# GpSimd's gathers in an edge-message kernel: issued when their buffers are free, no longer when TensorE passes given points

## The chip, the cores and the metric

The kernel runs on one core of one Trainium2 chip. The metric is device time in microseconds (us), the median of several runs. A core has five engines that work side by side, each through its own instructions in a fixed order: TensorE (PE: matrix products; PEld is its weight load), VectorE (DVE), ScalarE (ACT), GpSimd (POOL) and SyncE (SP, which only starts transfers). They wait for each other through semaphores. Transfers (DMA) run on 16 DMA engines and are started by SP, ACT or POOL.

## The reference

It is one layer of a graph network over 12,500 nodes of 32 features and 400,000 edges, which are sorted by their target node:

```python
h = jnp.maximum(_layernorm(x, axis=-1), 0.0)            # 12500 x 32
e_feat = jnp.concatenate([h[src], h[dst], edge_attr])   # per edge: 3 x 32 = 96
v = relu(e_feat @ W1 + b1) @ W2 + b2                    # 96 -> 64 -> 32
x_cand = jax.ops.segment_max(v, dst, num_segments=num_nodes)
out = x + jnp.maximum(x_cand, h)
```

## The kernel before, in words

**Tiling.** The edges are cut into four stripes of 100,000, and the four stripes lie on the 128 partitions, 32 features each. A chunk is 512 edges of every stripe, so 2048 edges; there are 196 chunks (`NCH`). A chunk has 16 columns (`K`) of 128 edges. Before the main loop the kernel normalises the nodes and writes `h` to memory as `h_d`, together with `q_d`, its product with the target part of `W1`.

**Two ways to fetch the source rows `h[src]`.** Of a chunk's 16 columns, 12 are fetched by POOL: one indirect DMA per column (`DMA_INDIRECT gh<-h_d,src_i`, line 179), which reads 128 rows of 128 bytes. The other 4 columns (`MM`) are looked up by TensorE instead: `tile(c, m)` multiplies a one-hot matrix `hot` with the node table `hs` in 14 matmuls of 448 columns (line 344), then DVE multiplies the result with a mask (`one<-pv,mask`, line 351) and takes a maximum (`gm<-one`, line 352). In 34 of the chunks (`MMX`) TensorE looks up a fifth column, `tile(c, MM)`, and POOL fetches 11.

**Buffers of the gathers.** POOL's columns land in tiles `gh` of three columns each, four tiles per chunk. The pool `gathered` has 14 such tiles. DVE turns each with one `STREAM_TRANSPOSE ht<-gh` (`to_features`, line 368), and after that the tile may be filled again: a gather's first column waits for the transposition of the tile 14 places earlier. Each gather also waits for the landing of the gather eight places earlier, since eight semaphores (`DMASW0` to `DMASW7`) take turns.

**The main loop.** It goes over pairs of chunks, 97 rounds. With c the pair that is finished, a = c+2 and b = c+3 are the chunks whose columns are fetched by TensorE in that round. On TensorE a round is, in this order: `ph<-ea` (the products with `edge_attr`, line 773), `ph<-of,qf` (with the target's part), `ph<-ht` (with the transposed source rows, `rows_into`), the transpositions `pv<-ident,sb` of the pair before (line 669), the tiles a1, a2, a3, the second layer `pv<-hid` (line 807), the product `pv<-so,last` that picks the last edge of each node (line 686), the tiles b0 to b3 (and the fifth tile, if there is one), and tile a0 of the next round. DVE transposes the gathered columns tile by tile between its work on TensorE's tiles. In one round it transposes eight `gh` tiles (a1 to a3, b0 to b3 and the next round's a0), and the next round's `rows_into` multiplies what it has transposed.

**What sets the order.** The kernel runs under a schedule written by hand: each engine carries out its instructions in the order of the program text. POOL's queue has nothing but gathers in the main loop. The gathers of chunks a+2 and a+3 stand at the end of a round's text, but POOL runs ahead of that as far as its waits allow. Those waits are the buffers, the eight semaphores, and, before the change, points of TensorE's order: `passes(round, name, ins)` remembers the instruction after which TensorE has passed a point, and `hold(c, i, ins)` makes gather i of chunk c wait for one. The table `HELD` names the points: of the 24 gathers of a pair every second one has a point. The first four points (`b1`, `b2`, `b3`, `n0`: the tiles b1, b2, b3 and the next a0) are of three pairs back, the other eight (`ea`, `ht`, `tr`: the three blocks of that name and the transpositions; `a1`, `a2`, `a3`; `lv`, which is the product of line 686; `b0`) of two pairs back. A second, short table `SOON` names points for the first gathers of chunks 3, 4 and 5; those points lie in the prologue.

Of the kernel before, what the change touches and what calls it, by code (L numbers as in the profile page):

```python
# [37 lines left out]
K = C // D  # L38
# [10 lines left out]
MM = 4  # L49
# [14 lines left out]
LATE = NCH - 8  # L64
PIECE = 2 * A0
GP = 3
HELD = {0: (3, 'b1'), 2: (3, 'b2'), 4: (3, 'b3'), 6: (3, 'n0'), 8: (2, 'ea'), 10: (2, 'ht'), 12: (2, 'tr'), 14: (2, 'a1'), 16: (2, 'a2'), 18: (2, 'a3'), 20: (2, 'lv'), 22: (2, 'b0')}
BANKS = 7
SOON = {(3, 0): 'a0', (3, 6): 'a2', (4, 0): 'a3', (4, 6): 'b0', (5, 0): 'b1', (5, 6): 'b2'}
ROUND = 12582912.0  # L70
# [13 lines left out]
def gnn_kernel(ctx, tc, x, src, src_mm, src_x, src_t, dst, dst_ext, lo, lo_c, ends_b, edge_attr, weights, w1, w2, b2, out):  # L84
# [88 lines left out]
    def gather(c):  # L173
        n = min(K - MM * (c in MMC), (SE - c * C) // D) - (c in MMX)
        parts = []
        for k in range(0, n, SOME):
            parts.append(gathered.tile([P, SOME, D], F32, name="gh"))
            for i in range(min(SOME, n - k)):
                ins = nc.gpsimd.indirect_dma_start(  # L179
                    out=parts[-1][:, i, :], out_offset=None, in_=h_d[:, :],  # L180
                    in_offset=bass.IndirectOffsetOnAxis(ap=src_i[:, c, k + i:k + i + 1], axis=0))
                hold(c, k + i, ins)
        return parts
# [33 lines left out]

    def hold(c, i, ins):

        at = HELD.get(i + c % 2 * (K - MM))  # L220
        if at and c // 2 - at[0] >= 0:
            waiting.append((ins, (c // 2 - at[0], at[1])))
        if (c, i) in SOON:
            waiting.append((ins, (0, SOON[c, i])))

    waiting = []
# [336 lines left out]
    with tc.tile_pool(name="edges", bufs=3) as pool, tc.tile_pool(name="edges_ps", bufs=1, space=PSUM) as ps:  # L563
# [290 lines left out]
        for c in range(0, NCH - 4, 2):  # L854
# [14 lines left out]
            if c == LATE + 2:  # L869
                ea = pool.tile([P, LOAD * C], F32, name="ea", bufs=2)  # L870
# [123 lines left out]
        c = NCH - 4  # L994
# [192 lines left out]
```

## Time and profile before

| | |
|---|---|
| median of three runs | 3579.48 us (3571.26 to 3581.6) |
| time of the profiled execution | 3575.96 us |
| its span, first to last instruction | 3574.1 us |
| mean granted TensorE clock | 0.944 |
| busy: PE, DVE, POOL, ACT | 3241.7, 2223.2, 2207.4, 1578.5 us |

The views quoted further on are these. The page of the profile gives each engine's busy time, the chain of work that ended last, and groups of instructions: engine, operation, output and inputs, count, then busy time, mean duration in ns, and the idle time of the engine just before them with what ended it. A row of the timeline has start, duration, engine, line and operation, and in brackets the idle time before it. A view by line has count and durations (min/median/max in ns). A view by stretches has, for each window, the length, the busy time of PE, PEld, DVE, ACT and POOL with counts, the granted TensorE clock, the share of the DMA engines and GB/s.

### The profile page before, as it was taken

What the parts mean: (1) busy time and instruction counts of PE and PEld (TensorE: products, weight loads), DVE (VectorE), ACT (ScalarE), POOL (GpSimd) and SP (SyncE); (2) the same over time, 40 slices, a digit from 0 to 9 for tenths busy, and PEclk for the clock granted to TensorE, in tenths of its full rate; (3) what the DMA queues carried; (4) which work ended last, traced back from release to release, by engine and by line L of the source; (5) the groups of instructions that cost most, each with busy time, mean ns of one, the idle gap of its engine ahead of it and who ended that gap; (6) DMA issues with size and microseconds to landing.
All of it is one profiled execution on the core that took longest, in us unless ns stands there. A gap on an engine that the chain in (4) does not pass through costs nothing.

```text
span 3574.1 us, 55458 instructions
## 1 busy us (share of the span) xinstructions
PE 3241.7 (91%) x19141; PEld 2547.7 (71%) x19141; DVE 2223.2 (62%) x4215; ACT 1578.5 (44%) x2470; POOL 2207.4 (62%) x2337
## 2 busy tenths in 40 slices
PE   5899999989999998999999999989999999999987
PEld 3577777777777776777777767777777777777765
DVE  5456666666666666666666666656665666666655
ACT  3344444443534444444443434444444444444443
POOL 6666666665666666666666666666666666666662
PEclk8899999999999999999999999999999999999997
DMA  5322222222222222222222222222222222222222
GB/s 175 99 60 62 53 64 62 62 50 62 64 62 53 61 63 65 50 66 60 62 50 70 57 56 58 59 59 61 60 62 59 60 61 61 63 65 49 59 58 65
DMA packets 178819, 227.49 MB, mean 64 GB/s; under 512 B 109621, under 2 KB 150373, under 8 KB 165734
## 3 DMA queue, kind: packets, MB, share of 16 engines
q10 hardware_dynamic: 29828, 108.01, 9.6%
q0 software_dynamic: 74336, 38.21, 8.5%
q1 hardware_dynamic: 74370, 77.70, 7.0%
q8 instruction: 151, 2.47, 0.3%
q14 instruction: 134, 1.10, 0.1%
HBM read 212.23 MB, written 11.46 MB: 63 GB/s over the span
## 4 chain that ended last, share of the span: by engine, by line
PE 81%; issue 10%; DVE 6%; another core or an unknown queue 2%; SPq 1%; DMA 1%; ACT 1%; DVEq 0%; ACTq 0%
PE pv L344 60%; PE ph L773 10%; PE pv L686 4%; PE pv L669 3%; PE pv L807 3%; DVE hot L304 1%; DVE one L351 1%; DVE last L650 1%; DVE sm L815 1%; DMA top_d<-wo 0%; DVE ht L368 0%; SPq L616 0%; SPq L707 0%; SPq L625 0%
## 5 line engine op out<-in xcount | busy, mean ns | idle before, releaser
L179 POOL DMA_INDIRECT gh<-h_d,src_i x2291 | 2169.8, 947 | 1296.3 <-issue 560.0
L344 PE MATMUL pv<-hs,hot 128*128 128x448 f32 x10752 | 2373.0, 378 | 97.5 <-issue 83.9
L344 PEld LDWEIGHTS pv<-hs,hot 128*128 128x128 f32 x10752 | 2089.1, 196 | 345.7 <-issue 159.7
L351 DVE TENSOR_TENSOR one<-pv,mask 128x448 f32<-128x448 f32 x768 | 472.3, 615 | 1219.7 <-remote 464.7
L798 ACT ACTIVATE hid<-ph,wt 128x512 f32<-128x512 f32 x392 | 250.0, 688 | 1124.6 <-remote 498.2
L352 DVE TENSOR_REDUCE gm<-one 128x32 f32<-128x448 f32 x768 | 476.2, 620 | 26.5
L304 DVE TENSOR_TENSOR hot<-kb,consts 128x1024 fp32r<-128x1024 f16 (+1 forms) x379 | 447.5, 1199 | 0.0
L318 ACT ACTIVATE hot<-away,ones 128x512 fp32r<-128x512 f32 x582 | 421.6, 724 | 45.0 <-remote 26.1
L317 ACT ACTIVATE away<-kb,key_n 128x512 f32<-128x512 f16 x582 | 416.0, 715 | 0.0
L692 ACT ACTIVATE wo<-pv 128x256 f32<-128x256 f32 x95 | 36.6, 385 | 631.2 <-remote 439.2
L815 DVE TENSOR_TENSOR_SCAN sm<-pb,sm,pv 128x512 f32<-128x512 bf16 x195 | 243.6, 1249 | 16.5 <-remote 9.0
L686 PEld LDWEIGHTS pv<-so,last 128*128 128x128 f32 x768 | 107.5, 191 | 159.5 <-issue 148.5
L773 PE MATMUL ph<-ht,wt 32*64 32x512 f32 x1568 | 197.3, 618 | 21.0 <-issue 13.0
L686 PE MATMUL pv<-so,last 128*128 128x256 f32 x768 | 148.6, 304 | 74.3 <-issue 67.7
L368 DVE STREAM_TRANSPOSE ht<-gh 128x96 f32<-128x96 f32 x774 | 207.4, 269 | 1.2
L661 ACT ACTIVATE sb<-sm,wt 128x512 f32<-128x512 f32 x196 | 138.1, 715 | 138.7 <-issue 87.6
L669 PEld LDWEIGHTS pv<-ident,sb 128*128 128x128 f32 x782 | 91.8, 150 | 120.3 <-issue 95.1
L773 PE MATMUL ph<-of,qf 32*64 32x512 f32 x1552 | 147.6, 600 | 19.6 <-issue 17.5
L669 PE MATMUL pv<-ident,sb 128*128 128x128 f32 x782 | 126.4, 298 | 30.4 <-issue 24.4
L773 PEld LDWEIGHTS ph<-ht,wt 32*64 32x64 f32 x1568 | 62.7, 135 | 114.1 <-issue 98.5
L642 ACT ACTIVATE of<-of,ones 128x512 f32<-128x512 f32 x194 | 140.6, 725 | 6.3
L641 ACT ACTIVATE of<-db,below 128x512 f32<-128x512 int32 x194 | 137.4, 708 | 0.0
(115 smaller groups left out, 1328.2 us busy)
## 6 DMA issues: line engine op xcount, KB each, us to landing
ea<-in_edge_attr SPq DMA_DIRECT2D x49, 1024.0 KB
db<-in_dst_ext ACTq DMA_DIRECT2D x48, 1024.0 KB
gh<-h_d,src_i POOLq DMA_INDIRECT x2291
pb<-pen_d ACTq DMA_DIRECT2D x48, 512.0 KB
kb<-key_d ACTq DMA_DIRECT2D x47, 512.0 KB
top_d<-wo SPq DMA_DIRECT2D x752, 3.0 KB
qf<-q_d SPq DMA_DIRECT2D x392, 16.0 KB
q_d<-qs SPq DMA_DIRECT2D x6, 512.0 KB
```

The costliest lines, as they stand in the source:

```text
L179: ins = nc.gpsimd.indirect_dma_start(out=parts[-1][:, i, :], out_offset=None, in_=h_d[:, :], in_offset=bass.IndirectOffsetOnAxis(ap=src_i[ ...
L304: nc.vector.tensor_tensor(hot_of(c)[:, start:stop], keys[c][:, None, :].to_broadcast([P, n, MM * P]), key_ps[:, start:stop, None].to_broad ...
L317: nc.scalar.activation(away, keys[c], AF.Square, bias=key_n[:, k:k + 1])
L318: nc.scalar.activation(hot_of(c)[:, k], away, AF.Relu, bias=ones, scale=-1.0)
L344: ins = nc.tensor.matmul(po, hot[k], hs[:, part, k].rearrange("p f a -> p (f a)"), start=(k == 0 and part == 0), stop=(k == A1 - 1 and par ...
L351: nc.vector.tensor_tensor(one, of_group, mask[:, None, :].to_broadcast([P, D, A0]), op=ALU.mult)
L352: nc.vector.tensor_reduce(row, one, axis=AX.X, op=ALU.max)
L669: passes(c // 2 + 1, "tr", nc.tensor.transpose(px[:, j, :], sb[:, j * P:(j + 1) * P], ident))
L686: ins = nc.tensor.matmul(pw[:, x % n], last[x][:, j].rearrange("p s w -> p (s w)"), sos[x][0][:, j], start=(j == 0 and x < n), stop=(j == ...
L773: ins = nc.tensor.matmul(ph[s][x * HID:(x + 1) * HID], w[g], e[g], start=start, stop=stop)
L798: nc.scalar.activation(hid[k], of, AF.Relu, bias=b1c)
L815: nc.vector.tensor_tensor_scan(found[:, :n], loaded.pop(c)[2][:, :n], pv[:, :n], -LOW if before is None else before[:, C - 1:C], op0=ALU.a ...
```

## The change

The table `HELD` and the three lines of `hold` that use it are taken out. What is left of `hold` serves `SOON` alone.

```diff
-HELD = {0: (3, 'b1'), 2: (3, 'b2'), 4: (3, 'b3'), 6: (3, 'n0'), 8: (2, 'ea'), 10: (2, 'ht'), 12: (2, 'tr'), 14: (2, 'a1'), 16: (2, 'a2'), 18: (2, 'a3'), 20: (2, 'lv'), 22: (2, 'b0')}
...
     def hold(c, i, ins):
 
-        at = HELD.get(i + c % 2 * (K - MM))
-        if at and c // 2 - at[0] >= 0:
-            waiting.append((ins, (c // 2 - at[0], at[1])))
         if (c, i) in SOON:
             waiting.append((ins, (0, SOON[c, i])))
```

No instruction of any engine changes its place. What changes is what POOL waits for. In the middle of the program, the twelve gathers of one chunk stood so on POOL before (`DMASW` is the landing of the gather eight places back, `DVE` the buffer, `PE` the point of TensorE's order):

```order
L179 DMA gh_16348<-h_d_63,src_i_70 128x32 [waits DMASW0_49,DVE_49,PE_49]
L179 DMA gh_16348<-h_d_63,src_i_70 128x32 [waits DMASW1_49]
L179 DMA gh_16348<-h_d_63,src_i_70 128x32 [waits DMASW2_49,PE_49]
L179 DMA gh_16352<-h_d_63,src_i_70 128x32 [waits DMASW3_49,DVE_49]
L179 DMA gh_16352<-h_d_63,src_i_70 128x32 [waits DMASW4_49,PE_49]
L179 DMA gh_16352<-h_d_63,src_i_70 128x32 [waits DMASW5_49]
L179 DMA gh_16356<-h_d_63,src_i_70 128x32 [waits DMASW6_49,DVE_49,PE_49]
```

And the same gathers on POOL now:

```order
L178 DMA gh_16348<-h_d_63,src_i_70 128x32 [waits DMASW0_49,DVE_49]
L178 DMA gh_16348<-h_d_63,src_i_70 128x32 [waits DMASW1_49]
L178 DMA gh_16348<-h_d_63,src_i_70 128x32 [waits DMASW2_49]
L178 DMA gh_16352<-h_d_63,src_i_70 128x32 [waits DMASW3_49,DVE_49]
L178 DMA gh_16352<-h_d_63,src_i_70 128x32 [waits DMASW4_49]
L178 DMA gh_16352<-h_d_63,src_i_70 128x32 [waits DMASW5_49]
L178 DMA gh_16356<-h_d_63,src_i_70 128x32 [waits DMASW6_49,DVE_49]
```

Every second gather has lost its wait for PE; the first of every tile still waits for its buffer. Over the whole program POOL's waits for PE go from 1146 to 11. At the start, in chunks 4 and 5, POOL's order before was:

```order
L179 DMA gh_801<-h_d_63,src_i_70 128x32 [waits DMASW0_49,PE_49]
L179 DMA gh_805<-h_d_63,src_i_70 128x32 [waits DMASW1_49]
L179 DMA gh_805<-h_d_63,src_i_70 128x32 [waits DMASW2_49,PE_49]
L179 DMA gh_805<-h_d_63,src_i_70 128x32 [waits DMASW3_49]
L179 DMA gh_809<-h_d_63,src_i_70 128x32 [waits DMASW4_49]
```

And now it is:

```order
L178 DMA gh_801<-h_d_63,src_i_70 128x32 [waits DMASW0_49]
L178 DMA gh_805<-h_d_63,src_i_70 128x32 [waits DMASW1_49]
L178 DMA gh_805<-h_d_63,src_i_70 128x32 [waits DMASW2_49]
L178 DMA gh_805<-h_d_63,src_i_70 128x32 [waits DMASW3_49]
L178 DMA gh_809<-h_d_63,src_i_70 128x32 [waits DMASW4_49,PE_49]
```

Before, chunk 4's last tiles waited for `ea` and `ht` of the first round, and the points of `SOON`, which lie earlier, came for nothing behind them; now the first gather of chunk 5 waits for its point of `SOON`. The instructions of PE, DVE, ACT and SP, and what they wait for, are the same in both programs; 48 of PE's signals, which only POOL read, are gone.

## The prediction

> **What bounds the kernel now.** I read the page first: the busy times, the chain that ended last, then the groups that the change touches.
>
> ```profile
> span 3574.1 us, 55458 instructions
> ...
> PE 3241.7 (91%) x19141; PEld 2547.7 (71%) x19141; DVE 2223.2 (62%) x4215; ACT 1578.5 (44%) x2470; POOL 2207.4 (62%) x2337
> ...
> PE 81%; issue 10%; DVE 6%; another core or an unknown queue 2%; SPq 1%; DMA 1%; ACT 1%; DVEq 0%; ACTq 0%
> ...
> L179 POOL DMA_INDIRECT gh<-h_d,src_i x2291 | 2169.8, 947 | 1296.3 <-issue 560.0
> ...
> L368 DVE STREAM_TRANSPOSE ht<-gh 128x96 f32<-128x96 f32 x774 | 207.4, 269 | 1.2
> ```
>
> TensorE is busy for 91% and makes 81% of the chain; POOL is on the chain with nothing. POOL's output is read by one thing alone, the 774 transpositions, and the last row's last number is DVE's idle time in front of all of them together: 1.2 us. So no transposition waits for a gather in a way that counts, and a gather that comes earlier can save 1.2 us at the most.
>
> Next, what POOL waits for, longest first, and how far it is ahead. The second fence is the view by line of the first 1800 us: gathers issued, transpositions done, fifth columns done.
>
> ```profile
> POOL gh L179 <- issue: 560.0, 1760, 3.4
> POOL gh L179 <- remote: 289.8, 181, 3.5
> POOL gh L179 <- PE pv L344: 238.8, 147, 4.7
> POOL gh L179 <- PE pv L686: 64.4, 34, 2.1
> POOL gh L179 <- PE ph L773: 58.6, 33, 6.1
> ```
>
> ```profile
> L179 POOL DMA_INDIRECT gh<-h_d,src_i x1156: 939/947/1463, 53.2 to 1799.0; - x193
> ...
> L368 DVE STREAM_TRANSPOSE ht<-gh x380: 233/268/280, 92.4 to 1795.0; 128x96 f32<-128x96 f32 x190
> ...
> L352 DVE TENSOR_REDUCE gh<-one x17: 619/620/621, 382.1 to 1774.8; 128x32 f32<-128x448 f32 x17
> ```
>
> By 1800 us 380 tiles had been turned, with 380 x 3 - 17 = 1123 gathered columns in them, and 1156 had been issued: POOL was 33 columns or 11 tiles ahead, of 14 that exist. The points of TensorE's order do hold it: three tiles stand empty. Without them POOL fills all 14.
>
> **The change, part by part.** One pair from the middle, from the timeline (POOL and DVE):
>
> ```profile
> 1812.50 0.27 DVE L368 STREAM_TRANSPOSE ht<-gh 128x96 f32<-128x96 f32 x1
> 1812.79 0.95 POOL L179 DMA_INDIRECT gh<-h_d,src_i  x1 [0.30 <-issue]
> 1815.46 0.94 POOL L179 DMA_INDIRECT gh<-h_d,src_i  x1 [1.72 <-remote]
> ...
> 1824.04 0.62 DVE L351 TENSOR_TENSOR one<-pv,mask 128x448 f32<-128x448 f32 x1 [8.91 <-remote]
> 1824.28 0.94 POOL L179 DMA_INDIRECT gh<-h_d,src_i  x1 [1.62 <-remote]
> ...
> 1825.23 0.27 DVE L368 STREAM_TRANSPOSE ht<-gh 128x96 f32<-128x96 f32 x1
> ...
> 1833.22 0.95 POOL L179 DMA_INDIRECT gh<-h_d,src_i  x1 [1.75 <-PE pv L344]
> ```
>
> ```profile
> 1807.94:1819.66 11.72, 10.61 (x60) 4.59 (x60) 6.99 (x16) 2.53 (x4) 7.87 (x9) 0.72 0.37 72
> 1819.66:1831.00 11.34, 11.34 (x70) 9.41 (x69) 6.67 (x13) 5.09 (x8) 7.59 (x9) 0.99 0.31 88
> 1831.00:1844.30 13.30, 13.30 (x68) 12.46 (x67) 11.28 (x23) 8.30 (x13) 7.99 (x9) 1.00 0.23 57
> sum 36.36, PE 35.25 PEld 26.47 DVE 24.93 ACT 15.93 POOL 23.44; mean PE 11.75 PEld 8.82 DVE 8.31 ACT 5.31 POOL 7.81
> ```
>
> *When the gathers go.* A gather takes 0.947 us, and 0.30 us passes to the next even without a wait, so 1.25 us. The 24 of a pair need 30.0 of its 36.4 us, and 6.4 us are left as waits. Now they come as pauses of 1.6 to 1.75 us in many places. Afterwards only an empty tile lets POOL go on: eight transpositions a pair, each good for three gathers or 3.75 us. Five of them stand close together (b0 to b3, then the next a0 at 1812.50), so POOL works through a backlog, and its pause gathers where no tile comes free for long: between a0 at 1812.50 and a1 at 1825.23. Three tiles of lead are 3 x 36.4 / 8 = 13.6 us, so the gathers go some 12 to 14 us earlier in the round. Price on the path: nothing, as all that reads them is already late. I take 0, between -1.2 us (the idle time above) and 0.
>
> *Fewer waits on POOL, fewer signals from PE.*
>
> ```profile
> L179 POOLq EVENT_SEMAPHORE  x1525: 17/17/43, 61.2 to 3516.6; - x191
> ```
>
> About half of these separate waits go. POOL is no bound, since it still has to wait 6.4 us a pair: 0. On PE 48 matmuls no longer signal POOL. What a signal costs PE no row shows; the nearest is this one, 17 ns for the handling of a semaphore, so 48 x 17 ns = 0.8 us. I take 0, between -0.8 and 0.8 us.
>
> *The queues.* POOL's queue holds gathers alone, so nothing is passed. Their transfers are the same number and size; they may not come faster than one in 1.25 us, which is the rate inside each of today's runs. The DMA engines are busy for 0.23 to 0.37 of the three stretches above. A gather that lands later by some us is still covered by the lead of 11 tiles, 11 x 36.4 / 8 = 50 us; if that cover were gone, each late tile would hold DVE for as long as it is late.
>
> *The start.* The waits of 3.5 and 4.0 us that POOL has for the first round's `ea` and `ht` go:
>
> ```profile
> 103.68 0.94 POOL L179 DMA_INDIRECT gh<-h_d,src_i  x1 [3.52 <-PE ph L773]
> ...
> 134.90 0.94 POOL L179 DMA_INDIRECT gh<-h_d,src_i  x1 [4.02 <-PE ph L773]
> ```
>
> ```profile
> 127.49 2.52 PE L773 MATMUL ph<-of,qf 32*64 32x512 f32 x9 [14.79 <-issue]
> ```
>
> TensorE stands still for 14.79 us there, and POOL gathers through all of it today; three or four gathers more ahead of it add to the traffic once. I take 0, between -1 and +2 us (two gathers' time, if a load that TensorE awaits stands behind them).
>
> *Contention: does a busy POOL slow anyone?* This has no row of its own; it is bounded by how much the durations of DVE's instructions spread, whatever POOL did beside them.
>
> ```profile
> L351 DVE TENSOR_TENSOR one<-pv,mask x768: 583/624/628, 55.9 to 3537.4; 128x448 f32<-128x448 f32 x192
> ...
> L352 DVE TENSOR_REDUCE gm<-one x768: 619/620/623, 56.5 to 3538.0; 128x32 f32<-128x448 f32 x192
> ```
>
> ```profile
> L398 DVE TENSOR_TENSOR step<-di x14: 391/392/466, 79.4 to 3313.8; 128x224 f32<-128x224 int32 x14
> ```
>
> The maximum, 768 times, is always 619 to 623 ns, with POOL busy for 62% of the span: a spread of 4 ns. The product ahead of it spreads by 45 ns. What TensorE awaits before `rows_into` is DVE's work on the tiles b0 to b3. With the 45 ns put wholly down to POOL, that is at most 4 x 45 = 180 ns a pair; with the 4 ns, 16 ns. I take the row of the maximum, which reads and writes a full tile beside POOL and shows nothing: 0, and keep both ends.
>
> [...]
>
> *Sum.* 3575.96 us (the profiled execution; its span is 3574.1, with 1.9 around it) + 0 = 3575.96. That execution lies 3.5 us under the median, 3579.48, against which I forecast: 3579 us. A change of 0.3%, 10.7 us, is about what a measurement of this kernel can tell from none; the three runs lie 10.3 us apart.
>
> **The rivals.** What can turn a small delay into a large one is TensorE's clock:
>
> ```profile
> 1816.40:1819.80 3.40, 3.40 (x13) 2.62 (x12) 0.00 (x0) 2.34 (x5) 2.48 (x4) 0.50 0.35 77
> 1823.30:1826.70 3.40, 3.40 (x18) 3.10 (x17) 2.62 (x6) 1.55 (x3) 1.89 (x2) 1.00 0.32 94
> ```
>
> ```profile
> core 0: 3574.1 us, clock 0.944
> ```
>
> After TensorE's stalls around `rows_into` the granted clock is 0.50 for a stretch, and the mean of 0.944 costs 0.056 x 3574 = 200 us. PE is idle for 3574.1 - 3241.7 = 332 us. So one us of idleness goes with 0.6 us of lost clock, and I count a delay on the path 1.6 times. [...]
>
> *Slower: POOL now works just when DVE does.* POOL's pause moves into the stretch where DVE is idle anyway (8.91 us before 1824.04), so beside DVE's work on b0 to b3 POOL's share rises from 7.99 / 13.30 = 0.60 to 0.947 / 1.25 = 0.76. If that costs DVE time, TensorE gets its rows later. Price: up to 97 x 0.18 x 1.6 = 28 us, 3607; in the middle 14 us, 3593. It decides from 10.7 / 1.6 / 97 = 0.07 us a pair. For it: DVE and POOL's overlap does grow, and the chain has DVE with 6%. Against it: the 4 ns.
>
> *Faster: the same coupling with the other sign.* The stretch of `tr`, a1 to a3 gets emptier of gathers. If their three products get 45 ns shorter, that is 97 x 0.135 x 1.6 = 21 us, 3558; half of it is 3569. Against it: DVE is early there, as its 8.91 us of idleness say.
>
> *The change does nothing to POOL,* because the buffers hold it at the same points: 3579. Against it stand the 11 tiles of 14.
>
> **How the numbers follow.** Nothing on the path moves: 0.47, and 0.03 for POOL not moving, both within 0.3%: 0.50. Slower by over 0.3%: 0.32, more than faster, 0.18, since the overlap with DVE's late work grows and the emptied stretch is one where DVE has time. The likeliest case's own range is 3569 to 3590. The 8 in 10 reach to the ends of both rivals, 3558 and 3607, and 6 us beyond for the spread of runs, half of the 10.3: 3552 to 3613.
>
> **What would show it.** Right: the waits for PE vanish from POOL's rows; its idle time, 1296 us, stays about the same and sits in fewer, longer pauses ahead of a1; by 1800 us POOL is 13 or 14 tiles ahead; the transpositions' idle time stays near 1 us; the maximum stays at 620 ns and the clock near 0.944. Wrong: rows of DVE whose mean duration rises, gathers longer than 947 ns, or a mean clock that moves by more than 0.003, which alone is 11 us.

## The result, and the profile after

The changed kernel takes 4203.41 us (median of four runs, 4198.63 to 4223.99) where the kernel before takes 3575.37 us (four runs, 3568.51 to 3581.6). The ratio is 1.176, with a 95% interval of 1.170 to 1.182: 17.6% slower, where "no change" was predicted. The profiled execution took 4223.99 us, 648 us more than the profiled one of before.

The page of the profile after, in the order in which the page of before was read (a group's last numbers are busy time, mean ns of one, idle time just before):

```profile
span 4222.1 us, 54700 instructions
...
PE 3623.3 (86%) x19141; PEld 2623.8 (62%) x19141; DVE 2223.9 (53%) x4215; ACT 1577.3 (37%) x2470; POOL 2207.9 (52%) x2337
...
L178 POOL DMA_INDIRECT gh<-h_d,src_i x2291 | 2170.5, 947 | 1944.1 <-DVE ht L364 1224.3
...
L769 PE MATMUL ph<-ht,wt 32*64 32x512 f32 x1568 | 501.5, 882 | 276.9 <-issue 263.9
L348 DVE TENSOR_REDUCE gm<-one 128x32 f32<-128x448 f32 x768 | 476.3, 620 | 26.5
L769 PEld LDWEIGHTS ph<-ht,wt 32*64 32x64 f32 x1568 | 107.9, 168 | 594.9 <-issue 575.6
...
L769 PE MATMUL ph<-of,qf 32*64 32x512 f32 x1552 | 242.0, 617 | 79.3 <-issue 68.9
...
L364 DVE STREAM_TRANSPOSE ht<-gh 128x96 f32<-128x96 f32 x774 | 207.5, 269 | 1.2
```

What the prediction looked at is as it was. A gather takes 947 ns, the maximum on DVE 620 ns, and the transpositions are still idle for 1.2 us in all: no gather comes too late, and no instruction of DVE or POOL is longer. The time sits with TensorE, and there with the products `ph` (line 769). These are their rows in the kernel before:

```profile
L773 PE MATMUL ph<-ht,wt 32*64 32x512 f32 x1568 | 197.3, 618 | 21.0 <-issue 13.0
...
L773 PEld LDWEIGHTS ph<-ht,wt 32*64 32x64 f32 x1568 | 62.7, 135 | 114.1 <-issue 98.5
...
L773 PE MATMUL ph<-of,qf 32*64 32x512 f32 x1552 | 147.6, 600 | 19.6 <-issue 17.5
```

The clock is lower as well (0.944 before):

```profile
core 0: 4222.1 us, clock 0.878
```

The products `ph<-ht` grow by 304.2 us in busy time and by 255.9 us in the idle time ahead of them, `ph<-of` by 94.4 and 59.7: 714 us together, more than the whole loss. The idle time ends with "issue": TensorE waited for nothing that the profile shows. The view of the waits says the same, after and (last fence) before:

```profile
DVE one L347 <- PE pv L340: 1298.5, 241, 19.3
POOL gh L178 <- DVE ht L364: 1224.3, 219, 17.6
...
PEld ph L769 <- issue: 839.5, 960, 2.7
...
PE ph L769 <- issue: 339.7, 399, 2.2
```

```profile
PEld ph L773 <- issue: 242.1, 548, 15.7
```

In the timeline it looks like this. POOL gathers without a break, since 1794.79 us; from 1803.3 us on TensorE's weight loads and products come singly:

```profile
1804.80 0.95 POOL L178 DMA_INDIRECT gh<-h_d,src_i  x1 [0.30 <-issue]
1805.65 1.35 PE L769 MATMUL ph<-ht,wt 32*64 32x512 f32 x2 [0.81 <-issue]
1806.06 0.94 POOL L178 DMA_INDIRECT gh<-h_d,src_i  x1 [0.30 <-issue]
...
1806.37 0.13 PEld L769 LDWEIGHTS ph<-ht,wt 32*64 32x64 f32 x1 [1.97 <-issue]
1807.08 0.13 PEld L769 LDWEIGHTS ph<-ht,wt 32*64 32x64 f32 x1 [0.59 <-issue]
...
1810.61 0.18 PEld L769 LDWEIGHTS ph<-ht,wt 32*64 32x64 f32 x1 [1.28 <-issue]
...
1812.03 0.18 PEld L769 LDWEIGHTS ph<-ht,wt 32*64 32x64 f32 x1 [1.24 <-issue]
1812.31 0.95 POOL L178 DMA_INDIRECT gh<-h_d,src_i  x1 [0.30 <-issue]
...
1824.43 0.62 DVE L347 TENSOR_TENSOR one<-pv,mask 128x448 f32<-128x448 f32 x1 [18.01 <-PE pv L340]
...
1826.16 0.95 POOL L178 DMA_INDIRECT gh<-h_d,src_i  x1 [12.91 <-DVE ht L364]
```

The starts lie 0.7 us or twice that apart (1806.37 and 1807.08; 1810.61 and 1812.03). The view by stretches counts them (length; PE, PEld, DVE, ACT, POOL busy with counts; clock; DMA share; GB/s):

```profile
1794.79:1804.20 9.41, 7.61 (x60) 5.40 (x59) 9.27 (x20) 3.85 (x6) 7.27 (x8) 1.00 0.28 43
1804.20:1815.50 11.30, 6.15 (x8) 1.22 (x8) 2.22 (x3) 0.00 (x0) 6.92 (x8) 0.73 0.31 89
```

In the first stretch, from the run's first gather on, the view counts 60 + 59 = 119 instructions of TensorE in 9.41 us (three of them were under way when it began). In the second TensorE starts 16 in 11.30 us, one every 0.71 us, and the profile shows nothing that they wait for. The last gather of the run ends at 1813.26 us, and at 1815.5 us TensorE is back at its pace; but the clock has fallen (0.73 in that stretch), DVE has stood for 18.01 us, and POOL, out of empty tiles, stands for 12.91 us. Below this is called starving, and a starved stretch; it is the word for what the trace shows, not a cause.

### The profile page after: what moved, and what is told of

Its sections match the earlier page's. It is cut to its first block, busy times and chain, and to the rows that moved or that the text cites. A ratio compares the mean times of both kernels' runs of the same rounds, so it can differ in the third digit from the quotient of the medians.

```text
span 4222.1 us, 54700 instructions
## 1 busy us (share of the span) xinstructions
PE 3623.3 (86%) x19141; PEld 2623.8 (62%) x19141; DVE 2223.9 (53%) x4215; ACT 1577.3 (37%) x2470; POOL 2207.9 (52%) x2337
## 3 DMA queue, kind: packets, MB, share of 16 engines
q0 software_dynamic: 74336, 38.21, 6.8%
q8 instruction: 151, 2.47, 0.2%
q14 instruction: 128, 1.05, 0.1%
## 5 line engine op out<-in xcount | busy, mean ns | idle before, releaser
L178 POOL DMA_INDIRECT gh<-h_d,src_i x2291 | 2170.5, 947 | 1944.1 <-DVE ht L364 1224.3
L340 PE MATMUL pv<-hs,hot 128*128 128x448 f32 x10752 | 2329.0, 374 | 103.4 <-issue 76.1
L340 PEld LDWEIGHTS pv<-hs,hot 128*128 128x128 f32 x10752 | 2056.7, 194 | 318.0 <-issue 128.8
L769 PE MATMUL ph<-ht,wt 32*64 32x512 f32 x1568 | 501.5, 882 | 276.9 <-issue 263.9
L769 PEld LDWEIGHTS ph<-ht,wt 32*64 32x64 f32 x1568 | 107.9, 168 | 594.9 <-issue 575.6
L769 PE MATMUL ph<-of,qf 32*64 32x512 f32 x1552 | 242.0, 617 | 79.3 <-issue 68.9
L665 PEld LDWEIGHTS pv<-ident,sb 128*128 128x128 f32 x782 | 131.4, 197 | 144.4 <-PE ph L769 75.1
L769 PEld LDWEIGHTS ph<-of,qf 32*64 32x64 f32 x1552 | 62.5, 135 | 226.7 <-issue 217.8
L665 PE MATMUL pv<-ident,sb 128*128 128x128 f32 x782 | 167.5, 381 | 9.7 <-ACT sb L657 5.3
L682 PEld LDWEIGHTS pv<-so,last 128*128 128x128 f32 x768 | 96.9, 188 | 82.7 <-issue 82.7
```

The source lines that it names most:

```text
L178: ins = nc.gpsimd.indirect_dma_start(out=parts[-1][:, i, :], out_offset=None, in_=h_d[:, :], in_offset=bass.IndirectOffsetOnAxis(ap=src_i[ ...
L340: ins = nc.tensor.matmul(po, hot[k], hs[:, part, k].rearrange("p f a -> p (f a)"), start=(k == 0 and part == 0), stop=(k == A1 - 1 and par ...
L665: passes(c // 2 + 1, "tr", nc.tensor.transpose(px[:, j, :], sb[:, j * P:(j + 1) * P], ident))
L769: ins = nc.tensor.matmul(ph[s][x * HID:(x + 1) * HID], w[g], e[g], start=start, stop=stop)
```

## The experiments

Each kernel is the changed one with the edit shown, unless said otherwise. "Starved" is one measure for all: the sum of the gaps between two successive starts on TensorE (products and weight loads) that last 0.64 to 0.76 us or 1.33 to 1.46 us, that is, one or two steps of 0.7 us. The runs met several chips, and they differ: on some the kernel before takes 3575 to 3627 us (below, the first kind), on others 3003 (the second kind). So each time stands beside that of the kernel before on the same chip. Whether the difference belongs to the chip, or to a condition in which it was met, the runs don't tell: one chip was met twice, with e1 to e4 and with e12 to e15, and was of the first kind both times; each of the others that ran an experiment was met with one set of runs. All experiments but the last are single runs, and only differences of several per cent are read from them.

| run | edit | before, us | this, us | clock | starved, us |
|---|---|---|---|---|---|
| kernel before, profiled | | | 3575.96 | 0.944 | 272 |
| changed kernel, profiled | | 3575.96 | 4223.99 | 0.878 | 802 |
| e1_bufs11 | 11 tiles instead of 14 | 3627 | 4212 | 0.890 | 748 |
| e2_hold1 | one point, `tr` | 3627 | 4224 | 0.847 | 1018 |
| e3_ahead4 | all points, 4 gathers later | 3627 | 3627 | 0.944 | 356 |
| e4_pause | 4 us of fills a pair | 3627 | 4080 | 0.878 | 704 |
| e9_after | none | 3585 | 4192 | 0.881 | 788 |
| e10_nogather_again | fills for gathers | 3585 | 3035 | 0.987 | 36 |
| e11_spaced_again | one fill per gather | 3585 | 4188 | 0.883 | 779 |
| e12_direct_again | plain transfers | 3626 | 3038 | 0.985 | 39 |
| e13_break8_again | 1.6 us of fills per 8 | 3626 | 4007 | 0.890 | 438 |
| e14_half_bytes | 64 bytes a row | 3626 | 4191 | 0.890 | 795 |
| e15_break6_short | 0.8 us of fills per 6 | 3626 | 4154 | 0.883 | 546 |
| e5_nogather | fills for gathers | 3003 | 3006 | 0.991 | 1 |
| e6_direct | plain transfers | 3003 | 3006 | 0.990 | 0 |
| e7_spaced | one fill per gather | 3003 | 3018 | 0.990 | 1 |
| e8_break8 | 1.6 us of fills per 8 | 3003 | 3391 | 0.948 | 2 |
| e16_four_points | four points | 3003 | 3007 | 0.991 | 0 |
| e17_spaced_two | two fills per gather | 3003 | 3776 | 0.915 | 10 |
| e18_four_again | four points | 3004 | 3006 | 0.992 | 1 |

The fills are `nc.gpsimd.memset(counts, 0.0)`; `counts` is not read any more in the main loop, so they only take POOL's time, about 0.2 us each (eight take 1.56 us in e13).

### Is it the lead or the pattern? (e1, e3)

The points had done two things: they kept POOL from running 14 tiles ahead, and they broke up its gathers. e1 takes away the lead and leaves the points out:

```diff
-    gathered = ctx.enter_context(tc.tile_pool(name="gathered", bufs=14))
+GATHERED = 11
...
+    gathered = ctx.enter_context(tc.tile_pool(name="gathered", bufs=GATHERED))
+    const.tile([P, 14 - GATHERED, SOME, D], F32, name="fill")
```

> No points of TensorE's order, as in the changed kernel, but 11 gather tiles in place of 14 (the room of the other three is filled, so that nothing else moves). POOL can then be no further ahead than the 11 tiles of the kernel before. Theory A, the unbroken run: TensorE loses its time where its burst of small matmuls (ph, line 773) falls into a run of gathers that no wait breaks for more than some 8 us; the buffers alone still let such runs of 15 gathers happen, so the time stays at 4100 to 4300 us. Theory B, the lead: what costs is that three more tiles are filled, 12 us earlier; then the time goes back to 3560 to 3620 us.

e3 keeps every point and moves each to the gather four later, which lets POOL run four gathers further ahead in the same pattern:

```diff
+HELD = {0: (3, 'lv'), 2: (3, 'b0'), 4: (3, 'b1'), 6: (3, 'b2'), 8: (3, 'b3'), 10: (3, 'n0'), 12: (2, 'ea'), 14: (2, 'ht'), 16: (2, 'tr'), 18: (2, 'a1'), 20: (2, 'a2'), 22: (2, 'a3')}
```

> All twelve points, but each holds the gather four places later in the list, so POOL is four gathers (1.3 tiles, some 6 us) further ahead than before and as evenly spread. Theory A: the spread is what counts, 3560 to 3640 us. Theory B: the lead is what counts, and 1.3 of the 3 tiles of lead are taken, 3700 to 3900 us.

Measured: 4212 and 3627 us (before: 3627). The tile `fill` only keeps the addresses of the others as they were. Both times came out as theory A expected: three tiles less of lead bring nothing back, and four gathers more of it cost nothing while the points are there. So it is not the lead; what the points did was to break up the gathers.

### Is it the block `ph`? (e2)

In the changed kernel the starved stretches fall on `ph<-ht`. The first theory was that this block is what gathers must keep away from. e2 puts back a single point, which lets the run of gathers begin only after it:

```diff
+HELD = {12: (2, 'tr')}
```

> 14 tiles and one of the twelve points alone: gather 12 of each pair waits for TensorE's transpositions (tr) two rounds back, which stand right behind the ph stretch. Theory A: the run of 15 is cut before it reaches the ph stretch, 6 gathers ahead of it and 9 behind, so most of the loss goes: 3560 to 3700 us, and ph<-ht's matmuls are back near 200 us busy from 501. Theory B: the gathers of the first half still go as early as in the changed kernel, so at least half of the loss stays: over 3850 us.

Measured: 4224 us, outside of what theory A expected, and inside what its rival B did (over 3850). Its groups:

```profile
L344 PE MATMUL pv<-hs,hot 128*128 128x448 f32 x10752 | 2652.7, 397 | 665.2 <-issue 658.9
...
L773 PE MATMUL ph<-ht,wt 32*64 32x512 f32 x1568 | 128.4, 609 | 12.5 <-DVE ht L371 12.5
```

`ph<-ht` is cured (501.5 us busy and 276.9 idle went to 128.4 and 12.5), and the products of the look-up tiles, which had been idle for 103.4 us, are idle for 665.2 us instead. So it is not this block: in both kernels what TensorE has to do late in a long run of gathers is starved. Rival B put the loss down to how early the gathers of the first half go, which is the lead, and against that stand e1 and e3.

The place where it begins can be counted. From the first gather after the last pause of more than 1.5 us to the first slow start, TensorE has started, in the changed kernel, a median of 123 instructions in 72 such places (8 in 10 lie between 117 and 128); in e9 121 (113 to 127), in e1 118 (104 to 136), in e2 124 (119 to 132), in e11 123 (113 to 127), in e14 113 (104 to 118). It hardly depends on which instructions these are, or on the time that they take: with about the same count the median time to it is some 9 us in the changed kernel and some 11 us in e2. In the kernel before and in e3, whose pauses are many and short, no such number stands out: 8 in 10 places lie between about 80 and 250 starts, and between about 90 and 210.

### Would a pause of POOL help? (e4)

```diff
+REST = 20
...
+        if c >= 6 and c % 2 == 0:
+            for _ in range(REST):
+                nc.gpsimd.memset(counts, 0.0)
```

> No points, 14 tiles; after the twelfth gather of each pair POOL does 20 small memsets on a dead tile, some 4 us, and then goes on. POOL is as busy as ever but starts no transfer meanwhile. Theory A in its narrow form (the gathers' transfers or the writing of their lists do it): the run is cut by work that is no gather, 3560 to 3750 us. Theory C (any unbroken work of POOL does it): the loss stays or grows, 4100 to 4400 us. Theory B: 4100 us or more as well.

Measured: 4080 us, between the ranges of theory A (to 3750) and of C and B (from 4100), and close to the second. The pauses work as breaks: counted from the last pause in the gathers of over 1.5 us, fills or not, the starved stretches begin after a median of 117 starts (98 to 129), as elsewhere; counted from the last time that POOL had nothing to do, after 280. That points to the gathers, and not to POOL's being busy; e10 below shows it. But one pause a pair is too few.

### The same on a second kind of chip (e5 to e8, e9)

The next four kernels met a chip on which the kernel before takes 3003 us and nothing starves:

e5 has fills in place of the gathers:

```diff
-                ins = nc.gpsimd.indirect_dma_start(
-                    out=parts[-1][:, i, :], out_offset=None, in_=h_d[:, :],
-                    in_offset=bass.IndirectOffsetOnAxis(ap=src_i[:, c, k + i:k + i + 1], axis=0))
+                if c >= 6:
+                    ins = nc.gpsimd.memset(parts[-1][:, i, :], 0.5)
+                    for _ in range(REST):
+                        nc.gpsimd.memset(counts, 0.0)
...
```

with `REST = 5`; the first six chunks gather as before.

> No points, and from chunk 6 on every gather is replaced by six fills on POOL that take about as long as a gather (1.2 us together) and write a constant into the column, so the source rows are not fetched and the output is wrong. POOL's order, waits and time stay as in the changed kernel. Theory A (the gathers, run without a break, starve TensorE of instructions): the starvation goes, ph<-ht has an idle time below 50 us, the clock is 0.944 or more, 3300 to 3620 us. Rival B (POOL being busy for long, whatever it does): 4000 us or more, clock below 0.90.

e6 has plain transfers there:

```diff
+                if c >= 6:
+                    ins = nc.gpsimd.dma_start(out=parts[-1][:, i, :], in_=h_d[(k + i) * P:(k + i + 1) * P, :])
...
```

> No points, and from chunk 6 on every gather is replaced by a plain transfer that POOL starts, of 128 rows of 128 bytes that lie one behind the other, so the rows are the wrong ones and the output is wrong. If the transfers themselves (their packets, or their traffic) starve TensorE: 4000 us or more. If it is what POOL does for an indirect one (947 ns of work on addresses): as without gathers, 3300 to 3620 us. A plain transfer may be cheaper on POOL, which would spread the packets differently; then only a time near the changed kernel's says something.

e7 has a fill behind each gather:

```diff
+                if c >= 6:
+                    nc.gpsimd.memset(counts, 0.0)
```

> No points, but one short fill (0.2 us) on POOL behind every gather, so POOL has a gather every 1.45 us instead of every 1.25 and no longer pause. Theory A as it stands (only a pause of 1.5 us or more lets TensorE catch up): 4000 to 4250 us, since the runs stay unbroken. Rival C (the share of time with a gather in work decides, and each small gap gives some back): clearly less than the changed kernel, 3600 to 3950 us.

e8 has eight behind every eighth (`REST = 8`):

```diff
+                rests[0] += 1
+                if c >= 6 and rests[0] % 8 == 0:
+                    for _ in range(REST):
+                        nc.gpsimd.memset(counts, 0.0)
```

> No points, but after every eighth gather, wherever TensorE stands, eight short fills on POOL (1.6 us together), so no run of gathers is longer than eight, as in the kernel before. Theory A (run length decides): 3560 to 3750 us, clock 0.93 or more, ph<-ht with an idle time below 60 us. Rival D (it is the place in TensorE's round that the points gave to the pauses, not their being there): 4000 us or more.

Measured: 3006, 3006, 3018 and 3391 us, with 0 to 2 us of starving. Each lies below every range that its expectation named: those were drawn for a chip on which the kernel before takes 3627 us. They answer none of the questions, but two things come from them. e8 shows what its breaks cost where nothing starves: the row of the transpositions has 742.6 us of idle time now, so POOL had become the bound.

```profile
L371 DVE STREAM_TRANSPOSE ht<-gh 128x96 f32<-128x96 f32 x774 | 211.4, 273 | 742.6 <-DMA gh<-h_d,src_i 740.4
```

And e7 ran without any point at 3018 us. Run again on a chip of the first kind, the same kernel took 4188 us (e11); the changed kernel itself took 4192 us there (e9), as expected for such a chip. So it was not the edit of e7 that kept it free. The changed kernel met no chip of the second kind, so e7 stands for it.

> The changed kernel itself again, since the kernel before took 3627 us in the first four experiments and 3003 us in the second four, which ran on another chip and showed no slow feeding of TensorE at all. If the slow feeding belongs to some chips and not to others, then where the kernel before takes about 3003 us here, the changed one takes 2990 to 3030 us with a clock of 0.99; and where before takes 3550 us or more, it takes 4150 to 4250 us. If the second four were free of it only because of their own edits, the changed kernel takes 17% more than before on either.

> The same kernel as in the run with one short fill behind every gather. Where before takes 3550 us or more: theory A expects 4000 to 4250 us, since the runs of gathers stay unbroken; rival C (each small gap gives some back) 3600 to 3950 us. Where before takes about 3003 us: 3018 us again.

The clock and the block `ph<-ht` of this one kernel on the two chips, e7 first (L771 is line 771 of that kernel; the numbers are count, then min/median/max in ns):

```profile
core 0: 3015.9 us, clock 0.990
```

```profile
L771 PE MATMUL ph<-ht,wt x1568: 587/587/1112, 67.2 to 2997.1; 32*64 32x512 f32 x196
```

```profile
core 0: 4186.4 us, clock 0.883
```

```profile
L771 PE MATMUL ph<-ht,wt x1568: 584/1007/1111, 97.6 to 4168.5; 32*64 32x512 f32 x196
```

The median product takes 587 ns on the one and 1007 ns on the other. As a test of small gaps, e11 says nothing: its fill fitted into the 0.3 us that POOL leaves behind a gather anyway.

```profile
1859.71 0.95 POOL L178 DMA_INDIRECT gh<-h_d,src_i  x1 [3.35 <-DVE ht L366]
1860.66 0.16 POOL L182 MEMSET counts<- 128x53 f32 x1
1860.98 0.95 POOL L178 DMA_INDIRECT gh<-h_d,src_i  x1 [0.16 <-issue]
```

A gather came every 1.27 us instead of every 1.25 us, and theory A and rival C were not told apart by it.

### What the gathers cost in all (e10)

> The same kernel as in the run without gathers (fills in place of the gathers from chunk 6 on, so the source rows are missing and the output is wrong). Where before takes 3550 us or more: theory A (the gathers starve TensorE) expects below 3300 us; rival B (POOL being busy, whatever it does) 4000 us or more. Where before takes about 3003 us: 3006 us again, which tells nothing.

Measured, on the same chip as e9 and e11: 3035 us, clock 0.987, 36 us of starving. This is with the source rows missing. POOL is kept in work almost as long: the fills of a column take it 1.01 us, where a gather takes 0.95 us and the next comes after 1.25. In 86 places it went on for more than 128 of TensorE's starts without a pause of 1.5 us (in the changed kernel in 112), and TensorE kept its pace. So the gathers are the cause, and they cost the kernel before some 550 us as well (3585 against 3035); without its points it is 1157 us.

### What of a gather does it? (e12, e14)

> The same kernel as in the run with plain transfers (128 consecutive rows of 128 bytes, started by POOL in 0.54 us each; wrong rows, so the output is wrong). Where before takes 3550 us or more: if small packets of POOL's transfers starve TensorE, 3500 us or more, since their number is the same; if it is POOL's work on an indirect transfer, 3030 to 3100 us, as without gathers. Where before takes about 3003 us it tells nothing.

> Every gather from chunk 6 on fetches 128 rows of 64 bytes instead of 128, one packet each as before, and a short fill on POOL writes the other half of the column (other rows too, so the output is wrong). The fill is the same small gap as in the run with one fill behind every gather. If the bytes that the gathers move starve TensorE: at least a third of the loss against no gathers (some 1150 us) goes, so below 3850 us. If it is the number of rows, or POOL's work on them: 4100 to 4250 us.

The edit of e14:

```diff
-                ins = nc.gpsimd.indirect_dma_start(
-                    out=parts[-1][:, i, :], out_offset=None, in_=h_d[:, :],
...
+                if c >= 6:
+                    ins = nc.gpsimd.indirect_dma_start(
+                        out=parts[-1][:, i, :D // 2], out_offset=None, in_=h_d[:, :].rearrange("n (a f) -> (n a) f", a=2),
...
+                    nc.gpsimd.memset(parts[-1][:, i, D // 2:], 0.5)
...
```

Measured: 3038 us with plain transfers, 4191 us with half the bytes. The bytes are not it: half of them starve as much as all (795 against 788 to 802 us). The plain transfers have the packets in the same number and size and starve next to nothing (39 us): POOL's queue has 74,336 packets in the changed kernel, in e12 and in e14 alike, with 38.21 MB in the first two and 19.83 MB in e14. So the packets alone are not it either. But they are also issued differently, as the expectation had it:

```profile
L179 POOL DMA_DIRECT2D gh<-h_d x2243 | 1186.8, 535 | 1671.0 <-DVE ht L367 1355.2
```

At 535 ns each POOL is through with a tile's three in 1.6 us and then waits for the next empty tile, so there are no long runs at all. Whether it is the indirect addressing, or only the time for which POOL is at it without a break, e12 doesn't tell.

### Must the breaks come where TensorE stands? (e13, e15)

> The same kernel as in the run with eight fills (1.6 us) after every eighth gather. POOL then needs 34.8 us a pair and took 3391 us where TensorE was not starved, so it can be no faster than that. Theory A (a break of 1.5 us or more after at most eight gathers lets TensorE catch up, wherever it comes): 3400 to 3650 us. Rival D (it is the place of the breaks in TensorE's round): 3900 us or more.

> After every sixth gather four fills on POOL (0.8 us), half the pause of the run with breaks, so the gathers are broken more often and more briefly; POOL needs 33.2 us a pair, 3220 us in all. If 0.8 us is enough for TensorE to catch up: 3300 to 3650 us. If a break has to be about 1.5 us: 3800 us or more, since 0.2 us gave nothing back (4188 against 4192 us).

e15 is e8's edit with `rests[0] % 6` and four fills. Measured: 4007 and 4154 us. Both missed what theory A expected (3400 to 3650, 3300 to 3650) and lie where the rivals did: from 3900 us on if the place of the breaks counts (e13), from 3800 if a break has to be longer (e15). The short breaks of e15 (the gaps of over 0.5 us between the end of a gather and the next have a median of 1.34 us, and a quarter of them are below 0.91 us) hardly count as breaks: leaving them out, the starved stretches begin after a median of 128 starts (115 to 151) since the last pause of over 1.5 us. The longer breaks of e13 (median 1.72 us) clear in part: counted from them, starving begins after a median of 90 starts (19 to 119). This is one:

```profile
1863.31 0.94 POOL L181 DMA_INDIRECT gh<-h_d,src_i  x1 [0.30 <-issue]
1864.26 1.56 POOL L187 MEMSET counts<- 128x53 f32 x8
1865.97 0.95 POOL L181 DMA_INDIRECT gh<-h_d,src_i  x1
```

```profile
1868.48 0.19 PEld L347 LDWEIGHTS pv<-hs,hot 128*128 128x128 f32 x1 [0.84 <-issue]
1869.20 0.19 PEld L347 LDWEIGHTS pv<-hs,hot 128*128 128x128 f32 x1 [0.53 <-issue]
1870.61 0.51 PEld L347 LDWEIGHTS pv<-hs,hot 128*128 128x128 f32 x3 [1.22 <-issue]
```

Two or three microseconds behind a break of 1.7 us TensorE is starved again. The many short starved stretches of e13 show in the clock rather than in idle time: TensorE is idle in it for 4004.2 - 3645.4 = 359 us, hardly more than the 332 us of the kernel before, but its clock is 0.890 instead of 0.944.

The kernel before has breaks of a median of 1.58 us, no longer than e13's, and starves for 272 us instead of 438. What its breaks have that fills don't is that they end when TensorE has passed a point. If TensorE is held up, POOL stands still for longer. That is a theory, E, and rival D in another form; fewer points were to test it.

### Four points, and two fills (e16, e17, e18)

The kernel before, with

```diff
-HELD = {0: (3, 'b1'), 2: (3, 'b2'), 4: (3, 'b3'), 6: (3, 'n0'), 8: (2, 'ea'), 10: (2, 'ht'), 12: (2, 'tr'), 14: (2, 'a1'), 16: (2, 'a2'), 18: (2, 'a3'), 20: (2, 'lv'), 22: (2, 'b0')}
+HELD = {0: (3, 'b1'), 6: (3, 'n0'), 12: (2, 'tr'), 18: (2, 'a3')}
```

> The kernel before with four of its twelve points: b1, n0, tr and a3, one to every sixth gather. Runs of gathers are then about six long, as with the fills after every sixth or eighth gather (4154 and 4006 us), but the breaks end when TensorE has come so far, so POOL stands still for as long as TensorE is held up. Theory E (the breaks must follow TensorE): 3600 to 3850 us. Theory A' (only the length of the runs counts): 3950 to 4200 us, as with the fills. If every second gather needs a point: 3900 us or more too.

> The kernel with four points again (b1, n0, tr and a3, one to every sixth gather), since the chip of the last two showed no slow feeding of TensorE with any kernel (before took 3003 us). Where before takes 3550 us or more: theory E (the breaks must follow TensorE's progress) 3600 to 3850 us; theory A' (only the length of the runs counts, about six here as with the fills, which gave 4154 and 4006 us) 3950 to 4200 us. Where before takes about 3003 us: 3007 us again, which tells nothing on this.

Both met chips of the second kind: 3007 and 3006 us. With ten runs of it against thirteen of the kernel before, the ratio is 1.0005 (0.9995 to 1.0014). Where nothing starves, eight of the twelve points are worth nothing, to within 0.14%. On theory E this says nothing, and it stays open.

e17 is e7's edit with two fills:

> No points, and two short fills behind every gather. One fill had fitted into the 0.3 us that POOL leaves behind a gather anyway (a gather every 1.27 us instead of 1.25); with two it should be one in 1.45 to 1.5 us, 35 us a pair, which allows no less than about 3450 us. Theory F (each gather goes on for some 0.2 us behind what POOL's rows show, so that at one in 1.25 us a backlog grows, and TensorE is fed when it is gone): 3450 to 3700 us. Theories A' and E (runs without a break of 1.5 us, or breaks that don't follow TensorE, starve it): 3950 to 4250 us.

Measured: 3776 us on a chip of the second kind, where no starving was to be expected and there was hardly any (10 us): POOL had become the bound (the transpositions are idle for 1284.0 us, waiting for gathers). On theory F it says nothing.

## Why the prediction was wrong

The failed step is "*Contention: does a busy POOL slow anyone?*", the term that the prediction bounded by 4 ns and 45 ns a time and took as 0. It measured 648 us between the profiled executions: in long runs of gathers TensorE starts an instruction only every 0.7 us.

- What it bounded is right. The maximum on DVE takes 620 ns with POOL in unbroken runs, as before. But the step put its question to the durations of DVE's instructions alone, and there was no cost there. What the gathers slow down is how soon the next instruction of TensorE starts (16 starts in the 11.30 us from 1804.20 us on). Such a delay stands in the idle column, with "issue", and on the engine that bounds the kernel, 332 us of whose idle time the prediction left without a cause. Rows for it were in the trace of before. The plainest are the weight loads of the look-up tiles, in the kernel before and (second fence) in e10, on a chip of the first kind too but without the gathers:

```profile
PEld pv L344 <- issue: 200.6, 288, 3.3
```

```profile
PEld pv L346 <- issue: 1.6, 2, 1.1
```

  The row of the `ph` products, `PEld ph L773 <- issue`, has 242.1 us in the kernel before, and this where nothing starves (e18, on a chip of the second kind):

```profile
PEld ph L773 <- issue: 126.0, 480, 0.8
```

  So about half of it is there anyway. Its longest wait of before, 15.7 us, is no starving: it ends at 127.49 us, in the first rounds, and DVE and ACT stood still in that stretch as well. The step should have asked what TensorE waits for where it waits for nothing.
- "*When the gathers go*" came out as worked out. By 1800 us the changed kernel had issued 981 gathers and turned 318 tiles, so POOL was 981 - (3 x 318 - 14) = 41 columns or 13.7 tiles ahead:

```profile
L178 POOL DMA_INDIRECT gh<-h_d,src_i x981 | 929.7, 948 | 818.3 <-DVE ht L364 514.1 <-issue 269.6 <-DVE ht L367 18.3
...
L364 DVE STREAM_TRANSPOSE ht<-gh 128x96 f32<-128x96 f32 x318 | 85.1, 269 | 0.5
...
L348 DVE TENSOR_REDUCE gh<-one 128x32 f32<-128x448 f32 x14 | 8.7, 620 | 0.5
```

  The pause lies ahead of a1 (12.91 us before 1826.16), and the transpositions' idle time stayed at 1.2 us. "Price on the path: nothing, as all that reads them is already late" holds for the readers of the gathers, and TensorE's instructions are no readers of the gathers.
- "Its idle time, 1296 us, stays about the same": it grew to 1944.1 us, by 647.8 us, the whole of the loss, since POOL does the same work in a longer time.
- "*Fewer waits on POOL, fewer signals from PE*" and "*The queues*" show no cost in the trace after: the gathers take 947 ns, and no transposition is late. At "*The start*" no load is seen to come late, but TensorE's starts come singly there already: weight loads at 98.50, 99.93, 101.33, 102.73 and 104.13 us in the changed kernel, products at 131.05, 132.46 and 133.85 us in the kernel before.
- Of the rivals, "*Slower: POOL now works just when DVE does*" had the sign, by a mechanism that did not occur, and far too small a size (14 to 28 us, against 628 us between the medians). Its factor of 1.6 for the lost clock was also small: TensorE's idle time grew by 598.8 - 332.4 = 266 us and its busy time by 3623.3 - 3241.7 = 382 us, so a microsecond of idleness went with 1.4 more. Most of that is the clock: by the prediction's own measure the clock of 0.878 costs 0.122 x 4222 = 515 us, 315 more than the 200 of before (an estimate). Part of it is a matter of counting: in a starved stretch single products that take 0.6 to 1.1 us come 0.7 us or more apart, and PE reads as 6.15 of 11.30 us busy with eight products.
- What the prediction named as a sign of its being wrong, a mean clock that moves by more than 0.003, is what came: 0.944 to 0.878. The other two signs, longer rows of DVE and longer gathers, did not.

One cause beneath can be looked up: that a transfer of TensorE's instructions comes late. The page has a queue for the transfer of instructions with the same number and size in the kernel before, in the changed one and in e18:

```profile
q8 instruction: 151, 2.47, 0.2%
```

That is 2.47 MB / 151 = 16 KB a transfer, and 38,282 / 151 = 254 of TensorE's starts to each; that they are TensorE's own is an estimate from this. One took a median of 1.05 us in the changed kernel and 1.04 us in e18, and the same transfer landed at the same place in TensorE's order in both, to a median of one start (8 in 10 within 30). The starved stretches begin anywhere between two of them (8 in 10 between 6 and 218 starts behind the last). So these transfers are not late, and nothing here ties the starving to them.

What stays open is the cause beneath: why TensorE starts only one instruction in 0.7 us after about 120 of them in an unbroken run of gathers, why the points keep the kernel before from about half of the loss (550 of 1157 us are left), and why some chips are free of it. All times here come from executions that the profiler recorded, and whether TensorE would be starved without it, no run here shows.

## What to carry to other kernels

An engine that is off the critical path can still hold up the one that bounds the kernel, while its own instructions and those of the engine between the two take as long as before (here the gathers took 947 ns and the maximum on DVE 620 ns in both kernels, and 648 us were lost): before calling a denser stream on another engine free, look at how the bounding engine's starts are spaced beside that stream today, and at the waits that end with "issue". Waits that look like mere pacing may be what keeps such a stream in pieces; take away half of them first, and look at the granted clock and the idle time rather than at the durations. And where a kernel may run on any of several chips, try such an edit on more than one: dropping the points (with one fill behind each gather) cost 0.5% on one (3018 against 3003 us) and 17% on another (4188 against 3585 us).

## What the runs showed of the hardware that was not expected

- On the chips of the first kind, in unbroken runs of indirect gathers (128 rows each, one in 1.25 us), TensorE starts instructions at its usual pace until about 120 have started (medians of 113 to 128 in seven kernels), and then one every 0.7 us (16 in 11.30 us in the changed kernel), until the gathers pause. In e4 (20 fills a pair, some 4 us) that begins a median of 117 starts after the last pause of over 1.5 us, fills or not; behind the breaks of e13 (a median of 1.72 us) it begins after a median of 90, 8 in 10 between 19 and 119. The breaks of e15 (four fills; gaps with a median of 1.34 us, a quarter below 0.91) left 4154 us and 546 us of starving.
- Halving the bytes of each row doesn't change it (795 us of starving against 788 to 802); fills on POOL in place of the gathers, 1.01 us a column, don't cause it (36 us), nor do plain transfers with the same packets, which POOL issues in 0.54 us each (39 us).
- The transfers of instructions land at the same places in TensorE's order whether it is starved or not (a median of one start apart, 8 in 10 within 30), and take a median of 1.05 and 1.04 us.
- The kernel before takes 3003 us on some chips and 3575 to 3627 us on others. A kernel without the gathers takes 3006 us on the one kind and 3035 us on the other, so nearly all of the difference between the chips comes with the gathers.
